# Moving tile additions, norms and turns between the softmax steps of the last attention units, and router scores as float32 products on column strips

## The chip, the cores and the metric

The kernel runs on one core of one Trainium2 chip. The metric is device time in microseconds of one launch of the whole program, the median of the runs shown. Engines are named as in the profile: PE is TensorE (PEld its weight loads), DVE is VectorE, ACT is ScalarE, POOL is GpSimd, SP is SyncE, which only issues DMAs here.

## The reference

The layer is a cross-attention block followed by a mixture-of-experts block, both added to the residual stream. There are 32 sequences of 100 tokens, 3200 tokens in all, of width 512.

```python
h = layernorm(x)                                  # over 512
q, k, v = h @ WQ.T, ctx[:, :100] @ WK.T, ctx[:, :100] @ WV.T   # 16 heads of 32
p = softmax(where(causal, q k^T / sqrt(32), -inf))
x = x + (p v) @ Wfc.T + bfc
h = layernorm(x)
scores = softmax(h @ gate_w.T)                    # 16 experts
w, idx = top_k(scores over the 100 tokens, 12)    # per sequence and expert
expert(e) = ((gelu(h[idx] Wg.T) * (h[idx] Wu.T)) Wd.T) * w   # 1024 hidden
out = x + scatter_add(expert) + shared(h)         # shared: the same form, all tokens
```

The context is longer than 100 positions, but the causal mask leaves only the first 100 in use. All is in float32. The kernel gets float32 accuracy from the faster `float32r` products by splitting each operand into a high part and a rest and adding three products (`mm3`, line 49): high x high, high x rest, rest x high.

## The kernel before

**Attention.** The tokens are cut into 8 blocks of four sequences, and each block into 4 units of four heads, 32 units in all (`NU`). A unit's steps are spread over three turns of the loop, so that PE has other work while the softmax of a unit goes through DVE, POOL and ACT:

- `qproj` and `qkeep` project q for unit u (PE, then an ACT copy);
- `scores` (L240) makes 16 float32 products of 100x100 for unit u-1 on PE; `sm_max` (L251, DVE) adds the mask and takes row maxima, 16 steps of about 0.18 us a unit; `sm_sub` (L260, POOL) subtracts them; `sm_exp` (L264, ACT); `sm_sum` (L269 and L270, DVE) sums and inverts; `sm_mul` (L275, POOL) scales. All but the maxima go by halves of a unit;
- `turns` (L281, PE transposes) and `keeps` (L286, ACT copies to `pt`), four of each, turn the probabilities of unit u-2; `values` (L296) multiplies them with v, 16 float32 products, each on a strip of 32 PE columns; `y_keep` (L101 on ACT, L102 on DVE) splits the result, and SP stores it.

While the first 29 units run, the k and v projections are woven in between. The last three units have no such filler. There `last_units` (line 400) writes out by hand an order in which the first token groups of the feed-forward part are prepared between the softmax steps.

**Preparing a token group (`Prep`).** Tokens are taken in nine groups of three or two tiles of 128 tokens. For each tile: `load_x` (SP), `bias` (L1017, POOL: x plus the output bias), `fc` (PE: y times Wfc, 12 products into a bank), `add` (L1026, DVE: bank plus x), `stats` (L1032 and L1033, DVE), `rsqrt` (L1039 and L1040, POOL), `norm` (L1047, DVE), `store` (SP, for the later gather), and `turn`. A turn puts the normalised tile with features on the partitions and splits it into `xh` (ACT) and `xl` (DVE). There are two ways: `turn_pe` (L958 to L960: four PE transposes into a PSUM bank, ACT copy to `xh`, DVE difference to `xl`), and `turn_dve` (L969 to L971: rows read again from DRAM in quarters, turned by DVE into an SBUF tile `big`, which stays float32, then split from there). Group 0 is turned by PE inside `last_units`; groups 1 to 5 are turned by DVE, groups 6 to 8 by PE.

**Router.** `logits` makes the 16 router scores of a group: `gw` holds the high part of gate_w in columns 0 to 15 and the rest in columns 32 to 47, and eight float32r products (4 slices of features, times `xh` and `xl`) go into 64 partitions of one bank (L1081). ACT copies one half (L1084), DVE adds the other (L1085), `tokens` turns the sum by PE transposes (L1092), and DVE copies it into `LG`.

**Feed-forward.** `begin` starts the first gate and up products of group 0; then `run` goes through the nine groups with the shared expert's weights, and through the 16 experts. PE is fed by `gate_up` (24 products, tile name `gu`) and `down` (`dn`), and the steps of the next group's `Prep` are hung between them by tables (`mid`, `post`).

**What sets the order.** PE, ACT, DVE and SP issue in exactly the order in which the code emits instructions, and within the attention part POOL does so too. So a line that is moved in `last_units` is moved in the queue of each engine that it uses.

**PSUM.** In the attention part there are eight banks: two for projections (`ps_kv`, tile name `kv`; also used by `fc`, and by group 0's `logits` and `tokens`), four for the scores of one unit (`ps_sc`), and two (`ps_ms`, tile name `ms`) shared by the turns of the probabilities, `values` and group 0's turns. A new tile takes the bank that was released first in the code's order, and waits for its last reader.

Of the kernel before, what the change touches and what calls it, by code (L numbers as in the profile page):

```python
# [31 lines left out]
GMAX = 384  # L32
# [28 lines left out]
def attention(tc, K, F):  # L61
    nc = tc.nc
    with ExitStack() as ctx, ExitStack() as kvctx:
# [336 lines left out]
        def last_units(pr):  # L400

            gp = nc.gpsimd

# [28 lines left out]
            u = NU - 2  # L432
            scores(u - 1)
            y_keep(u - 3)
            F.chunk_load()
            pr.bias(0)
            maxes(u - 1)
            pr.bias(1)
            pr.add(0)
            pr.stats(0)  # L440
# [22 lines left out]
            pr.bias(2)  # L463
            pr.stats(1)
            maxes(u - 1)
            pr.rsqrt(1)
            qkeep(u, qproj(u))
# [9 lines left out]
            sm_mul(u - 1, 0)  # L477
            pr.norm(1)
            turns(u - 2, 2, 3)
            keeps(u - 2, 2, 3)  # L480
            sm_sum(u - 1, 1)
            sm_mul(u - 1, 1)
            pr.add(2)
            pr.stats(2)
            pr.turn(0)
            values(u - 2)
            pr.turn(1)
            F.chunk_cast(0, 1)
            pr.rsqrt(2)
            pr.store(1)  # L490

# [9 lines left out]
            values(u - 1)  # L501
            F.preps[1].fc(0)
            pr.norm(2)
            sm_exp(u, 0)
            sm_sum(u, 0)
            sm_mul(u, 0)
            sm_exp(u, 1)
            sm_sum(u, 1)
            sm_mul(u, 1)
            pr.turn(2)  # L510
            y_keep(u - 1)
# [112 lines left out]
class FeedForward:  # L624
# [4 lines left out]
    def __init__(self, tc, K, top):  # L629
        self.tc, self.K, self.nc = tc, K, tc.nc  # L630
        self.starts = [sum(GROUPS[:g]) for g in range(len(GROUPS))]
        self.sw, self.raws, self.asked, self.nxt = {}, {}, 0, 0
        self.pend = self.late = None
        self.preps = {}
        self.scat = {}

        def pool(name, bufs):
            return top.enter_context(tc.tile_pool(name=name, bufs=bufs, side="right"))

        wfp = pool("f_wf", 1)  # L640
        self.wfh = wfp.tile([128, NC4, D], FR, name="wfh")
        self.wfl = wfp.tile([128, NC4, D], FR, name="wfl")
        self.bfc = wfp.tile([128, D], F32, name="bfc")
        self.base = wfp.tile([128, 5], F32, name="base")
        self.gr = wfp.tile([128, NC4, NE], F32, name="gr")
        self.gw = wfp.tile([128, NC4, 64], FR, name="gw")
        self.LG = wfp.tile([128, T // 128, NE], F32, name="LG")
        self.stacks = [top.enter_context(ExitStack()) for _ in range(3)]

    def load_consts(self):  # L650
        nc, K, gw, gr = self.nc, self.K, self.gw, self.gr
        nc.sync.dma_start(self.bfc, K.bfc)
        nc.sync.dma_start(self.base, K.base)
        nc.sync.dma_start(gr, K.gwT)
        nc.gpsimd.memset(f32(gw), 0.0)

    def split_consts(self):
        nc, gw, gr = self.nc, self.gw, self.gr
        nc.scalar.copy(gw[:, :, 0:NE], gr)
        nc.vector.tensor_tensor(gw[:, :, 32:32 + NE], gr, f32(gw[:, :, 0:NE]), ALU.subtract)  # L660
# [301 lines left out]
    def turn_dve(self, x, i, g):  # L962

        nc, cs = self.nc, slice(i * 128, (i + 1) * 128)
        xh, xl = x
        if i == 0:
            self.tx = self.bigp.tile([128, NC4, GMAX], F32, name="big")
        w = self.tx[:, :, cs]
        nc.vector.transpose(w, g.rearrange("p j (f b) -> p b j f", b=NC4))  # L969
        nc.scalar.copy(xh[:, :, cs], w)  # L970
        nc.vector.tensor_tensor(xl[:, :, cs], w, f32(xh[:, :, cs]), ALU.subtract)  # L971

    def expert_sink(self, e):
# [18 lines left out]
class Prep:  # L992


    def __init__(self, F, g, pm, pt):
        self.F, self.pm, self.pt = F, pm, pt
        self.t0, self.nt = F.starts[g], GROUPS[g]
        self.xb, self.ps, self.mv, self.xn, self.gx = {}, {}, {}, {}, {}
        self.xh = None

# [59 lines left out]
    def turn(self, i):  # L1060
# [3 lines left out]
        if i in self.gx:  # L1064
            self.F.turn_dve(x, i, self.gx.pop(i))
        else:
# [8 lines left out]

    def logits(self):
        F, nc, n = self.F, self.F.nc, self.nt * 128
        lg = self.pm()
        for t, xx in enumerate((self.xh, self.xl)):
            for d in range(NC4):  # L1080
                nc.tensor.matmul(lg[0:64, 0:n], F.gw[:, d, :], xx[:, d, 0:n],  # L1081
                                 start=(t == 0 and d == 0), stop=(t == 1 and d == NC4 - 1))
        lt = F.yp.tile([NE, GMAX], F32, name="so")
        nc.scalar.copy(lt[:, 0:n], lg[32:32 + NE, 0:n])  # L1084
        nc.vector.tensor_tensor(lt[:, 0:n], lt[:, 0:n], lg[0:NE, 0:n], ALU.add)  # L1085
        self.lt = lt

    def tokens(self):
        F, nc, nt, t0 = self.F, self.F.nc, self.nt, self.t0
        tk = self.pm()  # L1090
        for i in range(nt):
            nc.tensor.transpose(tk[:, i * NE:(i + 1) * NE], self.lt[:, i * 128:(i + 1) * 128],  # L1092
                                F.K.ident[0:NE, 0:NE])
        nc.vector.tensor_copy(F.LG[:, t0:t0 + nt, :],
# [217 lines left out]
```

## Time and profile before

| | us |
|---|---|
| median of three runs | 1690.23 |
| lowest and highest | 1687.83, 1692.22 |
| the profiled execution | 1690.93 |
| its span, first to last instruction | 1688.8 |
| PE busy | 1668.2 |
| DVE busy | 923.6 |
| ACT busy | 679.8 |
| POOL busy | 625.1 |

The span is 2.1 us shorter than the profiled execution's own time, and this execution is 0.7 us above the median. Times inside a profile count from the start of its span. The last attention units take roughly 325 to 382 us; from 382 to the end the feed-forward part runs. A row of a group gives line, engine, operation, tiles (out<-in) and count, then busy time and the mean length of one. In the timeline the brackets give the idle time of the engine ahead of an instruction and what ended it. PE's matmuls are pipelined, so the length of one is longer than the pace at which they follow each other; paces are read from the chain or from starts. A float32 product that is not a transpose leaves two matmul records in the trace.

### The profile page before, as it was taken

The page shows a single profiled execution, that of the slowest core. Times are in us where ns is not written, and L with a number is a line of the kernel's source. Part 1 is how long each engine was busy: PE and PEld are TensorE (multiplying, and loading weights), DVE is VectorE, ACT ScalarE, POOL GpSimd, SP SyncE. Part 2 cuts the span into 40 slices and gives each one's busy share as a digit, 9 for nine tenths or more (in the row PEclk, how much of TensorE's full clock was granted, in tenths as well). Part 3 has the DMA queues.
Part 4 walks back from the last instruction along what each step waited for, and adds up shares of the span by engine and source line. Part 5 has one row for each costly group of instructions (what it writes and reads, how often), then busy time and mean ns, then how long its engine had stood idle before and what let it go on. Part 6 is the DMA issues. An engine that isn't in the chain of part 4 may idle for free.

```text
span 1688.8 us, 28043 instructions
## 1 busy us (share of the span) xinstructions
PE 1668.2 (99%) x10854; PEld 1532.8 (91%) x10854; DVE 923.6 (55%) x2208; ACT 679.8 (40%) x1088; POOL 625.1 (37%) x541
## 2 busy tenths in 40 slices
PE   8999999989999999999999999999999999999999
PEld 7998888879989999989899999999999999999998
DVE  4878777665433434344555555555555555555542
ACT  4556555453111111122334444444444444444442
POOL 3777777670111011010243444333344333344011
PEclk9999999989999999999999999999999999999999
DMA  6456454555222214211445554555565555555452
GB/s 213 151 170 187 155 160 146 182 177 171 97 83 94 76 68 142 85 44 42 142 155 160 165 167 141 161 153 151 163 168 144 158 160 150 161 163 156 134 165 63
DMA packets 106741, 237.46 MB, mean 141 GB/s; under 512 B 13777, under 2 KB 58034, under 8 KB 106608
## 3 DMA queue, kind: packets, MB, share of 16 engines
q1 hardware_dynamic: 93248, 209.98, 38.0%
q0 software_dynamic: 12944, 25.22, 7.9%
q8 instruction: 85, 1.39, 0.4%
q10 hardware_dynamic: 416, 0.48, 0.1%
q14 instruction: 48, 0.39, 0.1%
HBM read 181.90 MB, written 53.73 MB: 140 GB/s over the span
## 4 chain that ended last, share of the span: by engine, by line
PE 94%; DVE 2%; ACT 1%; POOL 1%; issue 1%; DMA 1%; ACTq 0%; POOLq 0%; DVEq 0%
PE gu L56 49%; PE dn L56 24%; PE kv L56 11%; PE m L56 3%; PE ms L281 2%; PE ms L296 2%; POOL p L260 1%; PE sc L240 1%; DVE p L251 1%; ACT pt L286 1%; PE m L1081 1%; PE ms L171 0%; DMA kD<-kk 0%; PE m L958 0%; DVE y L102 0%
## 5 line engine op out<-in xcount | busy, mean ns | idle before, releaser
L56 PE MATMUL gu<-xh,whl 128*128 128x384 f32 (+1 forms) x3200 | 643.7, 332 | 0.7 <-ACT xh L959 0.7
L56 PEld LDWEIGHTS gu<-xh,whl 128*128 128x128 f32 x3200 | 558.9, 188 | 17.8 <-ACT xh L959 0.9
L56 PE MATMUL dn<-whl,hh 128*128 128x512 f32 x1168 | 368.0, 396 | 0.0
L733 DVE TENSOR_TENSOR whl<-wraw,whl 128x1536 fp32r<-128x1536 f32 x142 | 249.7, 1759 | 206.1 <-ACT whl L732 184.6
L938 POOL DMA_INDIRECT gx<-xnD,iq x180 | 226.7, 1260 | 362.0 <-DVE big L969 301.9
L56 PE MATMUL gu<-xl,whl 128*128 128x384 f32 (+1 forms) x1600 | 337.2, 332 | 0.0
L56 PEld LDWEIGHTS gu<-xl,whl 128*128 128x128 f32 x1600 | 280.0, 188 | 0.1
L767 ACT CAST hh<-g 128x384 fp32r<-128x384 f32 (+1 forms) x200 | 100.9, 505 | 408.3 <-DVE g L764 375.5
L56 PEld LDWEIGHTS dn<-whl,hh 128*128 128x128 f32 x1168 | 215.8, 188 | 36.9
L764 DVE TENSOR_TENSOR g<-g,gu 128x384 f32<-128x384 f32 (+1 forms) x200 | 108.3, 542 | 247.6 <-PE gu L56 245.4
L732 ACT CAST whl<-wraw 128x1536 fp32r<-128x1536 f32 x142 | 209.7, 1477 | 65.0 <-PE dn L56 60.8
L56 PE MATMUL dn<-whl,hl 128*128 128x512 f32 x584 | 230.6, 395 | 0.0
L763 ACT ACTIVATE g<-gu 128x384 f32<-128x384 f32 (+1 forms) x200 | 96.2, 481 | 239.8 <-PE gu L56 239.1
L768 DVE TENSOR_TENSOR hl<-g,hh 128x384 fp32r<-128x384 f32 (+1 forms) x200 | 110.8, 554 | 114.4 <-ACT hh L767 113.9
L980 POOL DMA_INDIRECT out_dram<-x,isl x48 | 77.7, 1619 | 172.8 <-ACT x L979 163.1
L56 PEld LDWEIGHTS dn<-whl,hl 128*128 128x128 f32 x584 | 109.8, 188 | 26.2
L260 POOL TENSOR_TENSOR p<-p,mx 100x800 f32<-100x800 f32 x64 | 96.5, 1527 | 65.7 <-DVE mx L251 61.3
L275 POOL TENSOR_TENSOR p<-p,sm 100x800 f32<-100x800 f32 x64 | 101.1, 1582 | 5.7 <-DVE sm L270 4.8
L251 DVE CUSTOM_DVE_ANT_0 p<-sc,mask 100x100 f32<-100x100 f32 x512 | 95.4, 256 | 0.0
L1017 POOL TENSOR_TENSOR x<-x,bfc 128x512 f32<-128x512 f32 x23 | 30.9, 1364 | 158.2 <-DMA x<-x 86.6
L970 ACT CAST xh<-big 128x512 fp32r<-128x512 f32 x59 | 36.7, 622 | 101.2 <-DVE big L969 101.2
L269 DVE TENSOR_REDUCE sm<-p 100x8 f32<-100x800 f32 x64 | 63.1, 986 | 23.8 <-ACT p L264 23.7
(155 smaller groups left out, 1656.0 us busy)
## 6 DMA issues: line engine op xcount, KB each, us to landing
wraw<-wE SPq DMA_DIRECT2D x144, 768.0 KB
yD<-y SPq DMA_DIRECT2D x31, 400.0 KB
xt<-x SPq DMA_DIRECT2D x32, 200.0 KB
vD<-vt SPq DMA_DIRECT2D x25, 256.0 KB
kt<-kD SPq DMA_DIRECT2D x32, 200.0 KB
v<-vD SPq DMA_DIRECT2D x8, 800.0 KB
xnD<-xn SPq DMA_DIRECT2D x25, 256.0 KB
out_dram<-x SPq DMA_DIRECT2D x25, 256.0 KB
```

The costliest lines, as they stand in the source:

```text
L56: r = nc.tensor.matmul(out, t[0][a], t[1][b], start=(first and i == 0), stop=(last and i == n - 1))
L251: nc.vector.tensor_tensor_reduce(out=p[:, bb, h, :], in0=sc[:, h, cs], in1=mask, scale=ISCALE, scalar=NEG, op0=ALU.add, op1=ALU.max, accum ...
L260: nc.gpsimd.tensor_tensor(pv, pv, mx[:, :, None].to_broadcast([S, 8, S]), ALU.subtract)
L275: nc.gpsimd.tensor_tensor(pv, pv, sm[:, :, None].to_broadcast([S, 8, S]), ALU.mult)
L732: nc.scalar.copy(h, r)
L733: nc.vector.tensor_tensor(l, r, f32(h), ALU.subtract)
L763: nc.scalar.activation(g[:, 0:t], pg[:, 0:t], AF.Gelu)
L764: nc.vector.tensor_tensor(g[:, 0:t], g[:, 0:t], pu[:, 0:t], ALU.mult)
L767: nc.scalar.copy(hh[:, 0:t], g[:, 0:t])
L768: nc.vector.tensor_tensor(hl[:, 0:t], g[:, 0:t], f32(hh[:, 0:t]), ALU.subtract)
L938: nc.gpsimd.indirect_dma_start(out=g[:, k, :], out_offset=None, in_=self.K.xn.rearrange("t (a f) -> (t a) f", f=128), in_offset=bass.Indir ...
L980: ins = nc.gpsimd.indirect_dma_start(out=self.K.out, out_offset=bass.IndirectOffsetOnAxis(ap=r.isl[:, i:i + 1], axis=0), in_=o, in_offset= ...
```

## The change

The change has two parts.

In `last_units`: `add(0)` moves from behind the maxima of unit NU-3 to directly behind the scores, ahead of `bias(0)`, which is now added after it. `rsqrt(1)` moves ahead of the maxima of unit NU-2, and `norm(1)` from between the two softmax sums to directly behind the maxima; `store(1)` moves up with it. `turn(0)` is made through a `kv` bank instead of an `ms` bank, ahead of `add(2)` and `stats(2)`; `add(2)` comes behind `values`, `stats(2)` behind `turn(1)`. In the last unit `turn(2)` moves ahead of the second softmax half, and `fc(0)` of the next group from ahead of `norm(2)` to behind `turn(2)`.

In the router: where a group was turned by DVE (groups 1 to 5), `logits` multiplies the float32 tile `big` by the unsplit gate weights, padded to 32 columns, in four float32 products, each into its own strip of 32 partitions. The strips are not added there. ACT copies all 128 partitions, and `tokens` multiplies the copy by a stack of four identity blocks (`sel`), which turns and adds in one float32 product a tile. The groups turned by PE keep the eight products; their two halves are added in the same way, over 64 partitions. The DVE addition of L1085 is gone. The constants `base` and `gr` are wider, and `gr` is cleared by POOL before its load.

```diff
--- before.py
+++ after.py
@@ -399,7 +399,7 @@
 
         def last_units(pr):
 
-            gp = nc.gpsimd
+            gp, mt = nc.gpsimd, pr.pt
 
             def maxes(u):
                 for hb in range(2):
@@ -431,12 +431,12 @@
 
             u = NU - 2
             scores(u - 1)
+            pr.add(0)
             y_keep(u - 3)
             F.chunk_load()
             pr.bias(0)
             maxes(u - 1)
             pr.bias(1)
-            pr.add(0)
             pr.stats(0)
             pr.rsqrt(0)
             qkeep(u, qproj(u))
@@ -462,8 +462,9 @@
             pr.store(0)
             pr.bias(2)
             pr.stats(1)
+            pr.rsqrt(1)
             maxes(u - 1)
-            pr.rsqrt(1)
+            pr.norm(1)
             qkeep(u, qproj(u))
             F.ask(1, lambda: ps_kv.tile([128, D], F32, name="kv"))
             F.preps[1].load_x(0)
@@ -475,19 +476,20 @@
             pr.fc(2)
             sm_sum(u - 1, 0)
             sm_mul(u - 1, 0)
-            pr.norm(1)
+            pr.store(1)
             turns(u - 2, 2, 3)
             keeps(u - 2, 2, 3)
             sm_sum(u - 1, 1)
             sm_mul(u - 1, 1)
+            pr.pt = lambda: ps_kv.tile([128, D], F32, name="kv").rearrange("p (c t) -> p c t", c=NC4)
+            pr.turn(0)
+            pr.pt = mt
+            values(u - 2)
             pr.add(2)
+            pr.turn(1)
             pr.stats(2)
-            pr.turn(0)
-            values(u - 2)
-            pr.turn(1)
             F.chunk_cast(0, 1)
             pr.rsqrt(2)
-            pr.store(1)
 
             scores(u)
             y_keep(u - 2)
@@ -499,15 +501,15 @@
             turns(u - 1, 2, 3)
             keeps(u - 1, 2, 3)
             values(u - 1)
-            F.preps[1].fc(0)
             pr.norm(2)
             sm_exp(u, 0)
             sm_sum(u, 0)
             sm_mul(u, 0)
+            pr.turn(2)
+            F.preps[1].fc(0)
             sm_exp(u, 1)
             sm_sum(u, 1)
             sm_mul(u, 1)
-            pr.turn(2)
             y_keep(u - 1)
             pr.store(2)
             F.chunk_cast(0, 2)
@@ -641,8 +643,9 @@
         self.wfh = wfp.tile([128, NC4, D], FR, name="wfh")
         self.wfl = wfp.tile([128, NC4, D], FR, name="wfl")
         self.bfc = wfp.tile([128, D], F32, name="bfc")
-        self.base = wfp.tile([128, 5], F32, name="base")
-        self.gr = wfp.tile([128, NC4, NE], F32, name="gr")
+        self.base = wfp.tile([128, 5 + NE], F32, name="base")
+        self.sel = self.base[:, 5:5 + NE]
+        self.gr = wfp.tile([128, NC4, 32], F32, name="gr")
         self.gw = wfp.tile([128, NC4, 64], FR, name="gw")
         self.LG = wfp.tile([128, T // 128, NE], F32, name="LG")
         self.stacks = [top.enter_context(ExitStack()) for _ in range(3)]
@@ -651,11 +654,13 @@
         nc, K, gw, gr = self.nc, self.K, self.gw, self.gr
         nc.sync.dma_start(self.bfc, K.bfc)
         nc.sync.dma_start(self.base, K.base)
-        nc.sync.dma_start(gr, K.gwT)
+        nc.gpsimd.memset(gr, 0.0)
+        nc.sync.dma_start(gr[:, :, 0:NE], K.gwT)
         nc.gpsimd.memset(f32(gw), 0.0)
 
     def split_consts(self):
         nc, gw, gr = self.nc, self.gw, self.gr
+        gr = gr[:, :, 0:NE]
         nc.scalar.copy(gw[:, :, 0:NE], gr)
         nc.vector.tensor_tensor(gw[:, :, 32:32 + NE], gr, f32(gw[:, :, 0:NE]), ALU.subtract)
 
@@ -969,6 +974,7 @@
         nc.vector.transpose(w, g.rearrange("p j (f b) -> p b j f", b=NC4))
         nc.scalar.copy(xh[:, :, cs], w)
         nc.vector.tensor_tensor(xl[:, :, cs], w, f32(xh[:, :, cs]), ALU.subtract)
+        return self.tx
 
     def expert_sink(self, e):
         nc, tc, scat, r = self.nc, self.tc, self.scat, self.route
@@ -996,7 +1002,7 @@
         self.F, self.pm, self.pt = F, pm, pt
         self.t0, self.nt = F.starts[g], GROUPS[g]
         self.xb, self.ps, self.mv, self.xn, self.gx = {}, {}, {}, {}, {}
-        self.xh = None
+        self.xh = self.tx = None
 
     def load_y(self):
         F, n, t0 = self.F, self.nt * 128, self.t0
@@ -1062,7 +1068,7 @@
             self.xh, self.xl = self.F.xt_tiles()
         x = self.xh, self.xl
         if i in self.gx:
-            self.F.turn_dve(x, i, self.gx.pop(i))
+            self.tx = self.F.turn_dve(x, i, self.gx.pop(i))
         else:
             self.F.turn_pe(x, i, self.xn[i], self.pt())
 
@@ -1074,23 +1080,32 @@
                 self.F.K.xn[self.rows(i), a * 128:(a + 1) * 128].rearrange("(j i) f -> i j f", i=32))
 
     def logits(self):
+
+
         F, nc, n = self.F, self.F.nc, self.nt * 128
         lg = self.pm()
-        for t, xx in enumerate((self.xh, self.xl)):
+        if self.tx is not None:
+            k = 128
             for d in range(NC4):
-                nc.tensor.matmul(lg[0:64, 0:n], F.gw[:, d, :], xx[:, d, 0:n],
-                                 start=(t == 0 and d == 0), stop=(t == 1 and d == NC4 - 1))
-        lt = F.yp.tile([NE, GMAX], F32, name="so")
-        nc.scalar.copy(lt[:, 0:n], lg[32:32 + NE, 0:n])
-        nc.vector.tensor_tensor(lt[:, 0:n], lt[:, 0:n], lg[0:NE, 0:n], ALU.add)
-        self.lt = lt
+                nc.tensor.matmul(lg[32 * d:32 * d + 32, 0:n], F.gr[:, d, :], self.tx[:, d, 0:n],
+                                 start=True, stop=True)
+        else:
+            k = 64
+            for t, xx in enumerate((self.xh, self.xl)):
+                for d in range(NC4):
+                    nc.tensor.matmul(lg[0:k, 0:n], F.gw[:, d, :], xx[:, d, 0:n],
+                                     start=(t == 0 and d == 0), stop=(t == 1 and d == NC4 - 1))
+        self.lt = F.yp.tile([128, GMAX], F32, name="so")[0:k]
+        nc.scalar.copy(self.lt[:, 0:n], lg[0:k, 0:n])
 
     def tokens(self):
-        F, nc, nt, t0 = self.F, self.F.nc, self.nt, self.t0
+
+        F, nc, nt, t0, lt = self.F, self.F.nc, self.nt, self.t0, self.lt
+        k = lt.shape[0]
         tk = self.pm()
         for i in range(nt):
-            nc.tensor.transpose(tk[:, i * NE:(i + 1) * NE], self.lt[:, i * 128:(i + 1) * 128],
-                                F.K.ident[0:NE, 0:NE])
+            nc.tensor.matmul(tk[:, i * NE:(i + 1) * NE], lt[:, i * 128:(i + 1) * 128],
+                             F.sel[0:k], start=True, stop=True)
         nc.vector.tensor_copy(F.LG[:, t0:t0 + nt, :],
                               tk[:, 0:nt * NE].rearrange("p (i e) -> p i e", e=NE))
 
@@ -1299,7 +1314,8 @@
         "gwT": g[m + "gate_w"].T.reshape(128, NC4, NE),
         "ident": np.eye(128, dtype=np.float32),
         "mask": np.where(np.tril(np.ones((S, S), bool)), 0.0, -1e30).astype(np.float32),
-        "base": np.hstack([(rows % B) * S, np.arange(128)[:, None] // 32]).astype(np.float32),
+        "base": np.hstack([(rows % B) * S, np.arange(128)[:, None] // 32,
+                           np.tile(np.eye(32)[:, :NE], (4, 1))]).astype(np.float32),
     }
     arrays = {k: np.ascontiguousarray(v) for k, v in arrays.items()}
     nc = bacc.Bacc("TRN2", target_bir_lowering=False, num_devices=1)
```

## The prediction, on record before the run

> **What bounds the kernel now.** I read the page first, then the PE's waits by stretch, then the granted clock by stretch, then the chain and the timeline of the stretch that stood out. The page:
>
> ```profile
> span 1688.8 us, 28043 instructions
> PE 1668.2 (99%) x10854; PEld 1532.8 (91%) x10854; DVE 923.6 (55%) x2208; ACT 679.8 (40%) x1088; POOL 625.1 (37%) x541
> ...
> PE 94%; DVE 2%; ACT 1%; POOL 1%; issue 1%; DMA 1%; ACTq 0%; POOLq 0%; DVEq 0%
> ```
>
> TensorE is busy 99% of the span and makes 94% of the chain. So an edit counts only if it takes work from PE, or takes a PE wait. The waits of PE from 345 to 400 us, where the last attention units hand over to the feed-forward part (engine, line, what it waited for: us, times, longest):
>
> ```profile
> PE ms L958 <- DVE xl L960: 2.9, 1, 2.9
> PE gu L56 <- ACT xh L959: 0.7, 1, 0.7
> PE ms L958 <- ACT pt L286: 0.6, 1, 0.6
> ```
>
> After 400 us PE waits under 2 us in all. The 2.9 us wait has a larger consequence, which the busy times by stretch show (third column: PE busy; the figure after POOL is the granted clock):
>
> ```profile
> 354.00:356.00 2.00, 0.00 (x0) 0.00 (x0) 1.90 (x6) 0.00 (x0) 1.36 (x1) 1.00 1.07 376
> 356.00:358.00 2.00, 1.37 (x25) 1.25 (x28) 0.58 (x2) 0.58 (x2) 1.92 (x4) 0.91 0.25 96
> 358.00:360.00 2.00, 1.86 (x27) 1.49 (x20) 1.74 (x9) 1.07 (x4) 1.51 (x2) 0.50 0.00 0
> 364.00:366.00 2.00, 2.00 (x6) 1.52 (x5) 1.53 (x3) 0.87 (x1) 1.36 (x2) 0.50 0.00 0
> 366.00:368.00 2.00, 2.00 (x6) 1.53 (x6) 0.43 (x2) 0.00 (x0) 1.86 (x2) 0.53 0.00 0
> 368.00:370.00 2.00, 1.32 (x9) 1.06 (x8) 0.33 (x1) 0.95 (x3) 0.14 (x1) 1.00 0.00 0
> ```
>
> PE stands empty from 353.7 to 356.6, and from about 357.6 to 367.9 it runs at half clock while busy nearly all the time: 10.2 us of PE work at half speed, some 5 us lost. The timeline says why PE stood: turn(1) needs the bank that turn(0) used, and that bank's second reader, `xl`, is queued on DVE behind a norm, a softmax sum, an addition and statistics:
>
> ```profile
> 351.61 1.76 DVE L1047 TENSOR_SCALAR xn<-x,mv,rs 128x512 f32<-128x512 f32 x1 [0.19 <-POOL rs L1040]
> 354.42 0.64 DVE L1026 TENSOR_TENSOR x<-kv,x 128x512 f32<-128x512 f32 x1
> 355.92 0.66 DVE L960 TENSOR_TENSOR xl<-ms,xh 128x512 fp32r<-128x512 f32 x1
> 356.63 0.56 PEld L958 LDWEIGHTS ms<-ident,xn 128*128 128x128 f32 x4 [3.14 <-DVE xl L960]
> ```
>
> **What the Trainium skill says.** (1) "TensorE: Matmul & The Clock Gate", "What's actually happening": the array falls to half clock after an idle window of about 3.4 us, and returns after a busy one; windows run free. The trace agrees: PE was busy 1.0 us of the 3.4 us before the drop, and the drop lasted 10.2 us, three windows. In the window before that one PE was busy 2.3 of 3.4 us and the clock stayed. (2) Same page, Part 3, "The mechanism": products on different 32-column strips run together. The trace agrees for `values` (L296): starts come in rounds of four strips, 86 ns a round. (3) "FP8 and Floating Point Precision", "TensorE Precision Notes": true float32 takes four passes. The trace: 16 `values` products leave 32 records, and a round of 100 columns takes 86 ns, two passes. (4) "SBUF — State Buffer", "Who interferes with whom": VectorE and GpSimd share a port pair; the later one waits for a whole instruction. The trace agrees: the norm takes 0.55 us (median) but 1.76 and 1.81 us beside a GpSimd product.
>
> **The change, part by part.** *add(0) earlier.* It leaves the place behind the maxima, where fc(1) waited 0.8 us for it (338.2 to 339.0), and runs in DVE's gap near 333.5; it needs only fc(0), over at 333.4. bias(0) stays at 335.2 on GpSimd, now after it. I take 0: the next thing late is GpSimd, which works without a gap from 340.0 to 345.4 and sets norm(0) (end 344.0), hence add(1) and all of DVE to 349.1. At most 0.8 gained.
>
> *rsqrt(1) and norm(1) earlier.* rsqrt(1) takes 0.87 us on GpSimd (350.71 to 351.58); it moves before the two subtractions, where GpSimd sat idle 1.1 us. norm(1) then starts on DVE at 349.1, after the maxima, in DVE's idle 1.15 us: 0.55 us, or until 350.75 if the subtraction of 349.21 takes the ports first; then the next sum starts 0.6 us late, still earlier than before. store(1) goes earlier with it: SyncE's order of DMAs stays the same (nothing of SyncE's lies between), so nothing is queued newly behind it.
>
> *turn(0) through a kv bank.* No wait: that bank's reader is the q copy at 347.4. From there on I walk through with the durations of this trace (us): sum 350.2 to 351.4; turn(0) 351.4 to 351.95; ScalarE ends both pt copies at 352.9, xh at 353.5; second sum 352.1 to 353.3; xl(0) to 354.2; values waits 1 us for pt, 353.0 to 353.85; turn(1) to 354.4, in a bank freed by pt; scores to 355.3. DVE: add(2) to 354.9, xl(1) to 355.7, statistics to 356.6, y to 357.2, maxima (2.9) to 360.1. So there are new waits of PE: turns(u-1) about 0.5 for xl(1) and 1.1 for y, 0.6 for pt. None is 2 us long.
>
> *turn(2) ahead of the next group's fc(0).* Queued behind turn(2) on PE is fc(0), 2.8 us, then gate_up. turn(2) waits for norm(2). GpSimd's two weight subtractions end 3.6 us after the statistics, DVE reaches norm(2) 3.4 to 3.5 us after them: if norm(2) gets in before the softmax subtraction, it ends at 360.5, otherwise at 361.7. turn(2) ends 0.55 later, fc(0) takes 2.8 at full clock, and gate_up starts at 363.9 or 365.1, since xh(2) is then ready under fc(0), so that its 0.7 wait goes too. Before it starts at 369.69. Gain 5.8 or 4.6; I take 5.2. The tail from there to the second gate_up (8.75 us) keeps its length; GpSimd's and ScalarE's casts are through in time. PE never waits for DMA in this stretch, so the later start does not come back elsewhere.
>
> *Router scores.* Only the five groups turned on DVE change (one of two tiles, four of three). Rows of the chain:
>
> ```profile
> 530.50 1.39 PE m L1081 x8
> ...
> 536.05 0.28 PE m L1092 x3
> ```
>
> Before: 1.39 us (two-tile group 0.92). After: four strips at once, two rounds of two passes. From `values`, 86 ns for 100 columns, a round of 384 is 0.33, of 256 is 0.22; and about 0.09 us at entry and at exit, as between `values` and its neighbours. So 0.84 and 0.62: gain 4 x 0.55 + 0.3 = 2.5. Not shown: the strips with 128 rows and 384 columns. Bounds: no entry cost, 3.4 gained; strips one after another, 8 x 0.33 + 0.18 = 2.8 and 1.9 us, 4 x 1.4 + 1.0 = 6.6 lost. I take 2.5, since `values` has the same form in groups of four. No accumulation order or reader is added: the wait is for the DVE turn, earlier than xh and xl.
>
> *Tokens.* Transposes of 16 rows become float32 products of 128 rows, two records each: per three tiles six weight loads. Before three take 0.28 and the following down product 0.2 more (2.30 against 2.10), with 0.06 per load. After 6 x 0.06 = 0.36, at most 6 x 0.12 = 0.7 (the pace of the 128-wide turns). Over nine groups between 1 gained and 2 lost; I take 0. The DVE addition, 0.54 us in most groups, goes; DVE is not the bound, so 0. The ScalarE copy has 128 partitions instead of 16: copies of 128x384 take 0.5 as this one did (0.47): 0.
>
> *Constants.* A GpSimd memset of 0.3 us at most (the similar one took 0.305), a load of gr in shorter runs that waits for it on SyncE, ahead of y and kv transfers. Both are issued at 164, gr is used at 184.5: 0, at most 0.5.
>
> Sum: 5.2 + 2.5 = 7.7 us. The profiled execution took 1690.93 (span 1688.8), 0.7 above the median 1690.23; on the median this gives 1682.5.
>
> **Rivals.** *A: the clock drops all the same.* The new waits lie among turns and scores from 352 to 362; if a window catches PE at no more than the 1.0 us of before, it drops. With norm(2) late, the worst 3.4 us holds about 0.9 us of work; otherwise 1.5. For: windows run free. Against: most positions hold 2 us. Two windows at half speed cost 3.4, three 5; I take 4: 1686.5. *B: the strips don't overlap.* Loss 6.6 against the stage's 5.2: slower, 1691.6. It decides from 2.5 us per three-tile score step. For: longer columns were never seen. Against: rounds of `values`. *C: the wait only moves.* DVE and GpSimd are the chain here (DVE 1.9 busy in each 2 us); if both norms lose the ports and the copies slip, gate_up starts near 367: stage gain 2.5, total 5.0: 1685.2.
>
> **How the numbers follow.** Forecast 0.54, A 0.22, B 0.10, C 0.14. Its own band is 1679 to 1685. Up to 1688 the range takes in C and nearly all of A; B is left out, and a little below 1679. About 0.3% (5 us) is what can be told from no change: faster is the forecast and half of C, with a little lost at the edge, 0.6; slower by that much needs B with A, 0.06; the rest 0.34.
>
> **What would show it.** The 2.9 us wait of turn(1) gone; clock 1.0 from 357 to 368; gate_up's start near 364.5; each wait in that stretch under 2 us; norm(1) near 349.1 with 0.55 us. Score steps of 0.84 us with four starts in a round; tokens of 0.3 to 0.4 us. A clock of 0.5 there, or score steps over 2 us, would make me wrong.

## The result and the profile after

| | before | after |
|---|---|---|
| median, us (runs) | 1690.36 (10) | 1683.88 (10) |
| lowest and highest | 1687.42, 1692.22 | 1681.56, 1686.37 |
| the profiled execution | 1690.93 | 1681.56 |
| its span | 1688.8 | 1679.3 |
| PE busy | 1668.2 | 1658.3 |

The ratio is 0.9964, with a 95% interval from 0.9955 to 0.9974: 6.5 us gained, where 7.7 were forecast. The total came out well, but its terms did not, as the experiments show. A second set of six runs of the changed kernel had a median of 1685.06 us (e10), so a difference of about 1 us between medians of different sets is not resolved. First the page after: span, busy time by engine, and the chain by engine.

```profile
span 1679.3 us, 28090 instructions
PE 1658.3 (99%) x10879; PEld 1523.6 (91%) x10879; DVE 919.0 (55%) x2199; ACT 679.5 (40%) x1088; POOL 625.2 (37%) x542
...
PE 93%; DMA 2%; DVE 1%; ACT 1%; POOL 1%; issue 1%; SPq 0%; ACTq 0%; POOLq 0%; DVEq 0%
```

PE is the bound as before. The waits of PE from 345 to 400 us (us in all, times, longest) show the first point of the forecast: the 2.9 us for `xl` is gone. A wait of 2.1 us for `xn`, the late norm(2), is new, where the forecast had every wait under 2 us; the rest are single waits under 1 us.

```profile
PE ms L963 <- DVE xn L1053: 2.1, 1, 2.1
PE ms L281 <- ACT pt L286: 1.1, 2, 0.8
PE ms L281 <- DVE y L102: 0.7, 1, 0.7
PE ms L281 <- DVE xl L965: 0.6, 1, 0.6
```

The timeline of after has norm(1) and norm(2), the subtraction of GpSimd beside the second, turn(2), fc(0) and the first gate_up:

```profile
348.51 0.58 DVE L1053 TENSOR_SCALAR xn<-x,mv,rs 128x512 f32<-128x512 f32 x1
358.84 1.91 DVE L1053 TENSOR_SCALAR xn<-x,mv,rs 128x512 f32<-128x512 f32 x1
358.93 3.20 POOL L260 TENSOR_TENSOR p<-p,mx 100x800 f32<-100x800 f32 x2
360.89 0.72 PE L963 MATMUL ms<-ident,xn 128*128 128x128 f32 x4 [2.06 <-DVE xn L1053]
361.37 1.17 PE L56 MATMUL kv<-wfh,yh 128*128 128x512 f32 x4
364.24 0.87 PE L56 MATMUL gu<-xh,whl 128*128 128x384 f32 x4
```

norm(1) took 0.58 us at 348.5, as forecast. norm(2) took 1.91 us beside the subtraction, so the branch of the walk with the late norm came true. The first gate_up starts at 364.24; everything in this trace lies 0.95 us earlier than before from the first exponential on, so this is 4.5 us gained in the stage, where that branch said 4.6. The busy times by stretch (third column PE busy, then PEld, DVE, ACT, POOL, then the clock) show no half clock here, though PE is far from full:

```profile
354.00:356.00 2.00, 0.79 (x18) 0.45 (x11) 1.93 (x5) 1.41 (x4) 0.59 (x3) 1.00 0.69 263
356.00:358.00 2.00, 1.63 (x24) 1.30 (x28) 2.00 (x24) 0.99 (x3) 2.00 (x3) 1.00 0.55 188
358.00:360.00 2.00, 0.83 (x32) 0.40 (x20) 2.00 (x13) 0.40 (x1) 2.00 (x2) 1.00 0.08 23
360.00:362.00 2.00, 1.11 (x7) 1.05 (x8) 1.34 (x2) 1.22 (x2) 2.00 (x2) 1.00 0.00 2
```

The router in the chain: a group turned by DVE (gate_up and down before; score step, gate_up, tokens, down after), then a group turned by PE (tokens, gate_up). Before:

```profile
531.89 4.16 PE gu L56 x24
...
536.34 2.30 PE dn L56 x9
...
729.06 0.28 PE m L1092 x3
729.34 4.38 PE gu L56 x24
```

After:

```profile
524.30 0.78 PE m L1090 x8
525.08 4.37 PE gu L56 x24
529.46 0.57 PE m L1107 x6
530.03 2.18 PE dn L56 x9
...
722.29 0.77 PE m L1107 x6
723.06 4.36 PE gu L56 x24
```

The score step fell from 1.39 to 0.78 us. But the gate_up behind it rose from 4.16 to 4.37, and tokens doubled from 0.28 to 0.57. In the group turned by PE, which keeps the old score products, tokens went from 0.28 to 0.77; the gate_up behind them was as long before (4.38). In the score step of after the starts of the four strips of a round lie within 0.02 us of each other.

Where the 9.5 us between the two profiled spans lie shows best in five stretches, each between starts of instructions in the timeline (us): to the first exponential (L264); from the 49th exponential to the first gelu (L763), the stage of the forecast; from the second gelu to the first of group 5; from there to the last gelu of group 8; and from the first expert's first gelu to the 15th's last. Kernels are named as in the experiments below.

| kernel | to first exp | stage | groups to 4 | groups 5 to 8 | experts |
|---|---|---|---|---|---|
| before | 47.15 | 89.34 | 271.64 | 234.41 | 749.14 |
| before, again | 45.96 | 89.02 | 271.67 | 234.46 | 749.14 |
| after | 46.20 | 84.61 | 270.04 | 235.26 | 746.36 |
| after, again | 46.98 | 85.32 | 270.04 | 235.45 | 746.36 |
| e2, router only | 46.25 | 88.98 | 270.01 | 235.20 | 746.36 |
| e5, addresses only | 47.07 | 89.18 | 270.89 | 233.77 | 746.36 |
| e8, fc(0) first, shifted | 46.61 | 85.72 | 269.14 | 235.24 | 745.73 |
| e9, e8 with the old router | 48.14 | 87.24 | 270.26 | 233.55 | 745.73 |
| e12, addresses, shifted | 45.93 | 90.17 | 270.25 | 233.53 | 745.73 |

The start differs by up to 2.2 us between executions and the stage by some too; the groups repeat within 0.2 us and the experts exactly. The experts are 2.78 us shorter after the change, and no line of the diff touches them.

### The profile page after: what moved, and what is told of

It is laid out like the page before. It is cut to its first block, busy times and chain, and to the rows that moved or that the text cites. A ratio compares the mean times of both kernels' runs of the same rounds, so it can differ in the third digit from the quotient of the medians.

```text
span 1679.3 us, 28090 instructions
## 1 busy us (share of the span) xinstructions
PE 1658.3 (99%) x10879; PEld 1523.6 (91%) x10879; DVE 919.0 (55%) x2199; ACT 679.5 (40%) x1088; POOL 625.2 (37%) x542
## 3 DMA queue, kind: packets, MB, share of 16 engines
q8 instruction: 85, 1.39, 0.4%
## 4 chain that ended last, share of the span: by engine, by line
PE 93%; DMA 2%; DVE 1%; ACT 1%; POOL 1%; issue 1%; SPq 0%; ACTq 0%; POOLq 0%; DVEq 0%
PE gu L56 49%; PE dn L56 24%; PE kv L56 11%; PE m L56 3%; PE ms L281 2%; PE ms L296 1%; PE sc L240 1%; POOL p L260 1%; DMA v<-vD 1%; DVE p L251 1%; ACT pt L286 1%; PE ms L171 0%; DMA kD<-kk 0%; DMA x<-x 0%; DMA yh<-yD 0%
```

## The experiments

### The parts: e1, e2, e4, and a first variant, e3

e1 is the kernel before with the new `last_units` alone. e2 is the changed kernel with the old `last_units`.

```diff
# e1 against before: last_units as in the change, nothing else
# e2 against after: last_units as before; its last lines
...
+            F.preps[1].fc(0)
             pr.norm(2)
...
-            pr.turn(2)
-            F.preps[1].fc(0)
...
+            pr.turn(2)
```

> The new order of the last units, with the router of the kernel before. If the stage brings nearly all of the gain (theory 1): 5 to 6 us faster than the kernel before, about 1684.5 to 1685.5, and the clock stays full from 350 to 370 us in most executions. If the router brings its forecast 2.5 us (rival): only 4 us faster, about 1686.4. The second gate_up starts near 373 us of the span either way.

> The old order of the last units, with the new router. Theory 1: the trace of the changed kernel shows score steps of 0.78 for 1.39 us, but the gate_up step behind them takes 0.2 longer and the token step with its down products 0.2 longer; so 0.2 us per three-tile group turned by DVE, less 0.2 for each group turned by PE: 0 to 1 us faster than before, 1689.5 to 1690.5. Rival: 2.5 us faster, 1687.9. The half clock near 358 to 368 us remains in both.

e1: 1687.92 (13 runs, before 1690.22), ratio 0.999 (0.9982 to 0.9998). e2: 1687.01 (13 runs), ratio 0.9982 (0.9974 to 0.9991). So the stage gave 2.3 us and not 5.2, less than either number expected of e1. The router's kernel gave 3.2 us: there theory 1 fell, and the rival's number was met. Its reason was still to be tested, since e2 also has the shorter experts.

e4 puts the four score products of a group into one strip, accumulated.

```diff
-            k = 128
+            k = 32
...
-                nc.tensor.matmul(lg[32 * d:32 * d + 32, 0:n], F.gr[:, d, :], self.tx[:, d, 0:n],
-                                 start=True, stop=True)
+                nc.tensor.matmul(lg[0:32, 0:n], F.gr[:, d, :], self.tx[:, d, 0:n],
+                                 start=(d == 0), stop=(d == NC4 - 1))
```

> The changed kernel, but the four score products of a group turned by DVE go into one strip and are added there, so that they can't overlap. If the strips overlap (theory): score steps of about 2.6 instead of 0.78 us and 1.8 instead of 0.57, so some 8 us slower than the changed kernel, about 1692. If the strips' overlap were not what makes the step short: the step stays under 1.5 us and the time within 2 us of the changed kernel.

It took 1696.28 us (4 runs), ratio 1.0041 (1.0026 to 1.0056), 12.4 above after's 1683.88 where 8 were expected; in its trace the groups to 4 are 10.1 us longer than in after, and the stage 2.5, with a drop of the clock. The same place of its chain:

```profile
532.28 2.70 PE m L1090 x8
534.98 4.36 PE gu L56 x24
539.34 0.77 PE m L1107 x6
```

2.70 against 0.78 us: on strips the products do overlap, and without that the forecast's bound of 2.8 holds. In e4 the starts of the eight records are 0.32 to 0.35 us apart. Rival B is out. The gate_up behind is as long (4.36) as behind four strips.

e3 puts fc(0) of the next group ahead of norm(2) and turn(2) again, as before the change, so that PE has work while norm(2) is late.

```diff
             values(u - 1)
+            F.preps[1].fc(0)
             pr.norm(2)
...
             pr.turn(2)
-            F.preps[1].fc(0)
```

> The changed kernel, with the next group's fc(0) put ahead of norm(2) and turn(2) again, as in the kernel before. If fc(0) behind turn(2) only moved PE's idle time (2.1 us for norm(2), against the 0.7 for xh before): fc(0) fills that wait, turn(2) starts at about 361.5 and gate_up near 362.7 to 363.4 instead of 364.2 us of the span, 1 to 1.5 us faster than the changed kernel, about 1682.5. And since no window is then nearly empty, no execution with a mean clock of 0.994 or 0.995. Rival: gate_up has to wait for xh, xl and the casts behind turn(2), and the time is the changed kernel's or up to 1 us more.

It took 1682.4 us (5 runs), ratio 0.996 (0.9946 to 0.9973): 1.5 under after's first median, which is too little to be sure. In its trace fc(0) fills the hole, and gate_up starts 1.3 us earlier than in after:

```profile
358.77 1.19 PE L56 MATMUL kv<-wfh,yh 128*128 128x512 f32 x4
...
361.67 0.63 PE L963 MATMUL ms<-ident,xn 128*128 128x128 f32 x4
...
362.98 0.97 PE L56 MATMUL gu<-xh,whl 128*128 128x384 f32 x4 [0.68 <-ACT xh L964]
```

### The addresses: e5

The wider `base` and `gr` lie in the pool below all right-hand tiles, so these (the transposed activations, `hh`, `hl`, weight buffers) lie 320 bytes lower in SBUF in the changed kernel, by the sizes in the program. e5 is the kernel before with only the two tiles enlarged; no instruction differs but in its addresses.

```diff
-        self.base = wfp.tile([128, 5], F32, name="base")
-        self.gr = wfp.tile([128, NC4, NE], F32, name="gr")
+        self.base = wfp.tile([128, 5 + NE], F32, name="base")[:, 0:5]
+        self.gr = wfp.tile([128, 2 * NC4, NE], F32, name="gr")[:, 0:NC4, :]
```

> The kernel before, with its two constant tiles of the router made as large as in the changed kernel and the added part unused, so that every SBUF tile on the right-hand side lies 320 bytes lower, as in the changed kernel; no instruction differs. The traces show the experts' stretch at 749.14 us in both kernels with the old tile sizes and at 746.36 in all three with the new. If the addresses make that difference (theory): 746.4 us again, and 2.5 to 3.5 us faster than the kernel before, about 1687. If the router's instructions make it (rival): 749.1 us and the time of the kernel before, 1690.2.

1685.41 us (8 runs, before 1690.12), ratio 0.9975 (0.9965 to 0.9986): 4.7 us from addresses alone, more than expected, with an interval from 2.4 to 5.9. The chain in the second of two experts, before and then e5 (start, us, what):

```profile
1069.33 4.24 PE gu L56 x24
1073.57 2.11 PE dn L56 x9
1075.68 4.24 PE gu L56 x24
1079.91 2.11 PE dn L56 x9
```

```profile
1068.65 4.16 PE gu L56 x24
1072.82 2.09 PE dn L56 x9
1074.91 4.24 PE gu L56 x24
1079.15 2.09 PE dn L56 x9
1081.24 4.16 PE gu L56 x24
```

The same 24 products take 4.24 us every time before, and 4.16 every second time in e5, with 0.02 off each down step. From expert to expert before alternates 50.18 and 50.57 us, e5 and after 50.13 and 50.23. By the table of stretches e5 has 1.4 us less in the groups and 2.8 in the experts, 4.2 in all.

### The bank and the order: e6, e7

e6 is the kernel before with only turn(0) sent through a `kv` bank, at its old place. e7 is after without that bank.

```diff
# e6 against before; e7 takes the same two lines out of after
+            pr.pt = lambda: ps_kv.tile([128, D], F32, name="kv").rearrange("p (c t) -> p c t", c=NC4)
             pr.turn(0)
+            pr.pt = mt
```

> The kernel before, where only turn(0) goes through a kv bank, in its old place in the order. If the missing bank made the wait (theory 1): turn(1) no longer waits for xl(0), starts at about 353.9 instead of 356.6 us, PE is never empty for more than 2 us in this stretch, and most executions keep the full clock: 1.5 to 3 us faster, 1687.5 to 1688.5. If DVE's order made it (theory 2): the 2.9 us come back in front of turns(u-1), which wait for xl(1) and y behind the same DVE queue, the clock still halves, and less than 0.7 us is gained.

> The changed kernel, where turn(0) goes through an ms bank again. Theory 2 (DVE's order is what counts): xl(0) is done near 353.4 us of the span, turn(1) starts 0.7 to 1 us later than in the changed kernel, and the time is within 1 us of it, 1683.5 to 1685. Theory 1 (the bank counts): PE waits 2 us and more for xl(0) again, the clock halves, and the time is 1686 or more.

e6: 1688.32 us (12 runs, before 1690.12), ratio 0.9991 (0.9982 to 0.9999), 1.8 gained. e7: 1686.48 us (8 runs), ratio 0.998 (0.997 to 0.999), 2.6 above after. By the medians the bank alone gives 1.8 us (0.2 to 3.0 by the interval) and the new order without it 0.5 (e2's 1687.01 less 1686.48). The traces do not show it the way theory 1 had it. The waits of PE in e6, then in e7:

```profile
PE ms L281 <- DVE xl L962: 2.2, 1, 2.2
...
PE ms L281 <- ACT pt L286: 2.2, 2, 1.9
PE ms L961 <- DVE xn L1051: 2.1, 1, 2.1
```

In e6 the wait for turn(0)'s bank is gone, but 2.2 us of waiting for `xl` stand in front of turns(u-1), where theory 2 had put them, and the clock still halves, for 6.8 us instead of 10.2. In e7 PE does not wait 2 us for `xl` at all, since the new order has DVE make xl(0) directly behind xh(0): its two long waits, for `pt` behind norm(0) and for `xn` behind norm(2), stand in e10 too, which has the bank (1.8 and 2.1). So theory 1's times came true in both, but neither trace shows its mechanism whole, and how much of e7's 2.6 us is the bank and how much the position of the clock's windows stays open. e7's clock falls twice, by the busy times in its windows of 3.41 us:

```profile
349.05:352.46 3.41, 1.50 (x9) 0.96 (x8) 2.76 (x20) 1.59 (x3) 3.15 (x2) 1.00 0.65 209
352.46:355.88 3.42, 3.21 (x36) 2.55 (x38) 1.95 (x5) 2.32 (x5) 2.64 (x3) 0.50 1.06 349
362.70:366.12 3.42, 1.35 (x15) 1.06 (x13) 2.77 (x6) 1.20 (x2) 3.42 (x3) 1.00 0.02 3
366.12:369.53 3.41, 3.41 (x10) 2.65 (x9) 2.71 (x6) 3.41 (x7) 2.61 (x3) 0.50 0.00 0
```

After 1.50 us of PE work in one window the next is at half clock, and again after 1.35.

### Both remedies, and the router by itself: e8, e9, e12

e8 is e3 with an unused tile of 32 bytes, which moves the right-hand tiles 32 bytes further. e9 is e8 with the router of before at the same addresses. e12 is the kernel before at the addresses of e8 and e9.

```diff
# e8 against e3; e12 against e5
         self.LG = wfp.tile([128, T // 128, NE], F32, name="LG")
+        wfp.tile([128, 8], F32, name="shift")
# e9 against e8: logits and tokens as before the change
```

> The changed kernel with fc(0) ahead of turn(2), and an unused tile of 32 bytes more among the constants, so that the tiles on the right-hand side lie another 32 bytes lower. If addresses set the pace of the products: the experts' stretch is another number than 746.36 us, the same for all experts of one kind of buffer, within 743 to 750. If the pace has nothing to do with addresses: 746.4 again and the time of the kernel with fc(0) first, 1682.4.

> The last units of the change (with fc(0) put ahead of norm(2) again) and the SBUF addresses of the shifted version, but the router of before: eight float32r products, DVE addition, PE transposes. Theory 1 (the new router's own instructions cost time, +0.55 us in the traces of layout-only and router-only, +1.6 us between their medians): this kernel is 0.5 to 1.6 us faster than the shifted version, so 1680.0 to 1681.0 at a median near 1681.5 of that one. Rival (the forecast's term: the score step is worth 2.5 us): it is slower than the shifted version, 1683.5 to 1684.

> The kernel before, with its right-hand SBUF tiles 352 bytes lower (320 as in layout-only, and 32 more); no instruction is changed. Theory 1 (addresses alone set the pace of the products in the experts and groups): 0.7 to 1.1 us faster than layout-only's 1685.4, so 1684.3 to 1684.8, and the stretch from the first expert's gelu to the last's near 745.7 us, where layout-only has 746.4 and the kernel before 749.1. Rival (the shifted version was faster than its parent by the router or by chance): 1685.4, the stretch unchanged at 746.4. From this run to the one with the old router and the new last units, at the same addresses, the stage alone remains: theory 1 expects 3 to 4.5 us between them.

e8: 1681.55 us (4 runs, before 1690.12), ratio 0.9949 (0.9934 to 0.9965). e9: 1680.66 us (5 runs, before 1690.7), ratio 0.9938 (0.9925 to 0.9952), 10.0 us under before and the lowest of all. e12: 1685.39 us (8 runs, before 1690.7), ratio 0.997 (0.9959 to 0.998).

Without the new router the median is 0.9 us lower, within theory 1's band; the intervals of e8 and e9 overlap, so by the times alone the sign is not sure, but the loss of 2.5 that the forecast's term asks for did not come. The stretches, which repeat better, give the sign: against e9 the new router wins 1.1 us in the groups to 4 and loses 1.7 in groups 5 to 8, and e2 against e5 wins 0.9 and loses 1.4.

For the second shift of 32 bytes the two measures disagree. The chain of e12 is now the same in every step,

```profile
1071.96 4.18 PE gu L56 x24
1076.15 2.08 PE dn L56 x9
1078.23 4.18 PE gu L56 x24
```

and its groups and experts are 1.5 us shorter than e5's. But the median did not move from e5's 1685.4: here the rival's number was met. The granted clock of the eight executions each accounts for it: on average 0.9948 in e12 and 0.9960 in e5, a difference that is worth about 2 us of a span of 1683 (an estimate from these figures). Whether that lower clock is chance is open. From e12 to e9, both compared with the same runs of before, the stage with fc(0) first gave 4.7 us.

### The same kernels again: e10, e11

e10 is the changed kernel and e11 the kernel before, each profiled a second time.

> The changed kernel, a second profile. If the length of norm(0) and the clock drop are chances of one execution: norm(0) is 1.8 or 3.2 us; a clock drop of 3.4 or 6.8 us near 353 to 366 is there with a chance of one in five, and then its time is 1686 and not 1683. If the changed order had removed the drop for good, there is none in this profile, and a mean clock of 0.997 or more. The median stays within 1683 to 1685.

> The kernel before, a second profile. If the windows of the clock run free of the program, the drop near 357 us need not last 10.2 us again: 3.4, 6.8 or 10.2 us, with a mean clock between 0.995 and 0.998 and a time from 1688 to 1691. If the drop is fixed by the order of the instructions, it is 10.2 us again, from 357 to 368.

e10: 1685.06 us (6 runs, before 1690.7), ratio 0.9967 (0.9954 to 0.9979), just outside the band expected; e11: one run, 1689.51 us. e11's drop lasted three windows again, 10.2 us, as in all five traces with the old order of the stage. It is the rule there and not a law: of the executions without a trace, one of 62 of before and one of 7 of e5 have a mean clock of 0.998, which leaves no room for 10.2 us at half clock (estimate: 5.1 us lost of some 1686, so at most 0.997). e11's window ahead of the drop and the first in it:

```profile
351.71:355.12 3.41, 0.92 (x33) 0.67 (x32) 3.31 (x7) 0.59 (x1) 1.85 (x3) 1.00 1.07 377
355.12:358.53 3.41, 2.98 (x38) 2.48 (x39) 1.35 (x3) 1.50 (x3) 2.58 (x4) 0.50 0.12 47
```

e10 had no drop, but norm(0) was other than in after's first trace. It met two products of GpSimd, and took 3.20 us instead of 1.81 (after, then e10):

```profile
341.63 1.81 DVE L1053 TENSOR_SCALAR xn<-x,mv,rs 128x512 f32<-128x512 f32 x1
...
342.16 3.20 DVE L1053 TENSOR_SCALAR xn<-x,mv,rs 128x512 f32<-128x512 f32 x1
...
342.08 3.01 POOL L275 TENSOR_TENSOR p<-p,sm 100x800 f32<-100x800 f32 x2
```

PE then stood nearly empty from 350 to 352 us, which it did not in after's first trace (1.56 busy):

```profile
350.00:352.00 2.00, 0.24 (x4) 0.24 (x4) 1.35 (x4) 1.61 (x3) 2.00 (x2) 1.00 0.80 225
```

The clock held there: e10's windows of 3.41 us divide the stretch at 350.60 and hold 2.83 and 2.03 us of PE work on its two sides, where other positions would catch as little as 1.45. e1, with the same order, has a window of 1.71 us and drops:

```profile
358.17:361.58 3.41, 1.71 (x38) 1.00 (x36) 3.41 (x25) 1.27 (x3) 3.41 (x3) 1.00 0.37 124
361.58:364.99 3.41, 2.75 (x9) 2.39 (x10) 2.62 (x5) 2.48 (x4) 2.77 (x3) 0.50 0.00 1
```

## Why the total was right and its terms were not

The runs form a path from before to after, one part at a time (medians, of sets whose runs of before differ by 0.1 to 0.2 us): the addresses take it from 1690.12 to 1685.41 (e5), 4.7 gained; the router's instructions to 1687.01 (e2), 1.6 lost; the stage to 1683.88, 3.1 gained. The forecast was 0 for the addresses, 2.5 gained by the router and 5.2 by the stage. A loss that it took for a gain, and a stage that gave less, were covered by a gain that it did not know. That the total of 7.7 came near the measured 6.5 was luck.

- **The bank and turn(1)**: the 2.9 us wait is gone, as forecast. With the bank alone (e6) 2.2 us of it came back one step later; with the order alone (e7) it did not show. By the medians the bank is worth more (1.8 against 0.5 us), but the traces do not say why.
- **norm(1), rsqrt(1), store(1)**: right in the trace (0.58 us at 348.5); no run separates their worth.
- **turn(2) ahead of fc(0)**: the walk held for the execution that was profiled (4.5 us for 4.6), since norm(2) was late, as its worse branch had it. But it put an empty PE in the place of fc(0), which e3 fills: the new wait of 2.1 us is the one that broke the forecast's "each wait in that stretch under 2 us".
- **Stage, the 5.2**: right in mechanism, off in size: 3.1 us by after less e2, 2.3 by e1. What failed is Rival A's condition, "if a window catches PE at no more than the 1.0 us of before, it drops". The Trainium skill ("TensorE: Matmul & The Clock Gate", "What's actually happening") says that the windows last 3413 ns and run free of the program, and here every stretch at half clock that ends within a span is one, two or three times 3.413 us. It gives no busy share that keeps the clock. In 14 traces, from 344 to 370 us, the last window at full clock ahead of a drop held 0.92 to 1.71 us of PE work, and 1.94 once (e9); those that kept the clock held 1.74 or more. So the border is well above 1.0.

  It is not sharp in the modelled busy time: near 11 to 15 us windows of 1.57 (e6) and 1.59 (e9) kept the clock, and at 166 us one of 1.80 dropped it in e5 and kept it in before. With the windows laid at every quarter microsecond over after's trace, 10 of 14 positions catch less than 1.75 us, the worst 1.35; over that of before all do; over that of e3 none does. So the order of the change keeps the clock only by luck of position. All five traces with the old stage dropped for 10.2 us. Of four with the new stage as changed, two dropped for 3.4 us and two not at all; of three with fc(0) first, e3 kept the clock, e8 dropped for 3.4 and e9 for 6.8. Where the clock held with the order of the change, the stage's stretch was 84.61 and 85.32 us, and 86.81 and 87.13 where it dropped once (e1, e4), against 88.98 to 90.17 with the old order.

  All executions together agree: the mean clock was 0.9958 in e2 and 0.9971 in after, worth about 2.2 us of a span of 1684 (estimate), where a drop of 10.2 us that is wholly gone would give 5.1. Rival A had a chance of 0.22; it was about even, with a smaller price (1.7 us for one window).
- **add(0) earlier, the 0**: not settled. With the old stage or the bank alone norm(0) took 1.81 us in six of six traces, with the new order 3.20 in six of eight; it starts 0.08 us behind GpSimd's product in either case. The skill ("SBUF — State Buffer", "Who interferes with whom") says that whoever issues first has the shared ports for a whole instruction. A norm takes 0.55 to 0.58 us alone, 1.81 beside one product and 3.20 beside two. The 1.81 agrees: there the two products together take 3.28 us (after), so the second waits for the norm. The 3.20 does not follow from it: there they take 3.01 (e10), and the second product goes ahead of a norm that is already waiting. Why it does so more often now, no run shows. e10's stage is 0.7 us longer than after's.
- **Router scores, the 2.5**: the size of the step itself was right (0.78 for 0.84 us, 0.57 for 0.62). What failed is that nothing behind it was charged: each next gate_up takes 0.2 longer. The skill ("TensorEngine Tiling (Array Packing)", "Tiling Modes") says that a change of the tiling mode drains TensorE. The 0.2 us fits that, but before pays it too behind its float32 transposes of 16 rows (gate_up 4.38, down 2.30) and not behind its float32r score products of 64 columns (4.16). That points to the float32 form; no run changed the one without the other.
- **Tokens, the 0**: failed, outside its bounds of 1 gained and 2 lost, with about 2.5 lost. Where DVE turned three tiles: 0.29 more, 0.12 given back by down. Where PE turned: 0.49 more in groups of three tiles, 0.33 in that of two. The pace taken from weight loads of 16 rows was too short: those take 0.13 us each, the new ones of 64 and 128 rows 0.19. In sum for a group of three tiles turned by DVE: -0.61 + 0.2 + 0.29 - 0.12 = -0.24 us; the group of two: -0.35 + 0.22 + 0.13 - 0.10 = -0.10. Four times -0.24, once -0.10, three times 0.49 and once 0.33 make 0.7 us lost. The stretches have 0.6 lost from the second gelu on, to which the 0.49 of group 0 comes; the medians have 0.9 (e8 less e9) and 1.6 (e2 less e5).
- **Constants, the 0**: failed. The load and the memset cost nothing that shows (242.5 us from the first exponential to the 49th, before and after); the 320 bytes that the wider tiles take were worth 4.7 us. The forecast looked at what the constants cost to load, and not at where everything above them goes.
- **Rival C**, the wait that only moves: norm(2) was late, as it feared, but norm(1) was not, and gate_up started at 364.2 in after. In e1, where norm(0) was late as well and the clock dropped once, it started at 366.8, close to the rival's 367, but by Rival A's means too.

Why addresses change the pace of TensorE, and which of the right-hand tiles do it, stays open: they were moved only together. A router with the new scores for groups turned by DVE and the old tokens for the others was not tried.

## What to carry to other kernels

When a change resizes a persistent tile, measure the resize alone before crediting the instructions: here it was worth more, by the medians, than either part that was meant. For a kernel bound by TensorE, count what a step does to its neighbours, and look for PE's emptiest window at every position, not at the one that a trace happened to show. Two profiles of one kernel tell which stretches repeat exactly and which are a matter of chance.

## What the runs showed that was not expected

- The pace of float32r products depends on the SBUF addresses of the tiles. Before, gate_up took 4.24 us in the experts, and these 50.18 and 50.57 in turn; with tiles 320 bytes lower 4.16 and 4.24, and 50.13 and 50.23; with tiles 352 bytes lower 4.18 and 50.13 every time.
- A drop of the clock follows a window that is half empty, not only one that is idle: of 3.41 us, windows with less than 1.57 us of PE work (modelled busy time) all dropped, those above 1.94 all kept the clock, and between the two both were seen. A drop lasts one to three windows, though PE is busy in them: 3.27 and 3.42 us in the first two of before's three, over 2.7 in the first of e6's two and e7's first two. What sets how many was not found.
- Three float32 products of 16 columns, two records each, take 0.77 us behind a down step and 0.57 behind gate_up, against 0.28 for PE transposes of 16 rows. The place alone does not decide: with 32 rows instead of 128 they take 0.77 behind gate_up as well (e4).
